# Bucketing an edge list on one core: lane products with the operands exchanged, packed moving rows, and rows turned back to columns by products

## The chip, the cores and the metric

The kernel runs on one core of one Trainium2 chip. The metric is device time in microseconds (us). The engines named here are PE (TensorE: matrix products, with PEld for its weight loads), DVE (VectorE), ACT (ScalarE), POOL (GpSimd) and SP (SyncE, which issues the transfers). In a product the stationary operand is loaded first ("weight load") and the moving operand is streamed past it.

## The reference

Four graph layers over the same 12500 nodes and 200000 edges, sorted by destination, each followed by a residual and a layer norm:

```
edge_index = stack([src, dst])
x = layernorm(x + L0(x, relation_emb, edge_index, edge_type))      # hyperbolic messages, 2 hops, mean per src
x = layernorm(x + L1(x, edge_index, edge_weight, msg_W, gru_...))  # 2 rounds: sum of messages per src, GRU
x = layernorm(x + L2(x, edge_index, W1_l, ...))                    # 2 x (segment_sum(h[src], dst)/deg @ W_l + b + h @ W_r)
x = layernorm(x + L3(x, edge_index, W1_l, ...))                    # the same, wider
```

Each layer gathers node rows by one end of the edges and sums them by the other. The change concerns only the preparation of the edge list, which all four layers use.

## The kernel before

Nodes are cut into 49 groups of 256 (`NG` = 49). An edge belongs to a cell (group of its destination, group of its source), and the program gives each cell 128 lanes. The function `fast` first writes two lists to DRAM: `l_code` (64 x destination group + source group) and `l_pay` (six bf16 numbers an edge: source, destination and edge type within their groups, each plus one, and the edge weight in three parts). Then it runs the **bucketing loop**, `for b in range(NG)`, L910 to L975: one pass for each destination group.

A pass takes a window of 4608 consecutive edges from the sorted list (128 partitions x `WC` = 36 columns) and does the following:

- DVE writes `og` (L919), which says for each edge and each of `GA` = 52 source groups whether it belongs there. Its layout is [partition, group, column], so that the 52 groups of one column lie 36 elements (72 bytes) apart.
- PE counts: `pc` (36 products, L923) the edges per column and group, and `pr` (L929 four products with `upto`, L932 thirty-six with `later`) the rank of each edge among those of its cell. ACT copies `pc` to `per` between the two.
- DVE multiplies `og` by `pr` into `m` (L935), takes the maximum over groups in six steps (L940) and gets `rank`, the lane of each edge. It writes `lane` (L948), which says for each edge and each of 128 lanes whether it goes there, in layout [partition, lane, column], and `v` (L951, six instructions), `og` times each payload number, in layout [partition, payload, group, column].
- PE does the **lane products** `po` (L954): 36 products, one a column, each with `lane[:, :, c]` stationary (128 columns) and `v[:, :, :, c]` moving (6 x 49 = 294 columns), which leaves payloads in [lane, payload x group].
- ACT takes one off (`cols`, L956), POOL writes `slc` and `dlc` (source and destination columns) and DVE adds the three weight parts in `ws`. PE turns `cols` by three transposes to `tr` (L968), ACT copies them to `hr` (L969), and after every seventh pass (`IG` = 7) SP stores `ws` and `hr` to `wgt`, `hop_rows`, `d_rows` and `s_rows` in DRAM.

The tile framework orders the instructions of the loop from its own estimate of costs. Each engine executes its list in order, so passes are interleaved as that order says. The buffers are two deep for `og`, `lane`, `v` and `po`, three for `code` and `pay`, and single for `m`, `pc`, `pr` and `tr`. When the loop is over, a flag is tested, and the layers follow: two hops of the first layer (until about 10.5 ms), then seven passes over all cells (`sum_pass`). They read what the loop has stored, and none of it is edited.

Of the kernel before, what the change touches and what calls it, by code (L numbers as in the profile page):

```python
# [11 lines left out]
F32 = mybir.dt.float32  # L12
BF16 = mybir.dt.bfloat16
I32 = mybir.dt.int32
I16 = mybir.dt.int16
AF = mybir.ActivationFunctionType
OP = mybir.AluOpType
# [6 lines left out]
P = 128  # L24
# [26 lines left out]
F16 = mybir.dt.float16  # L51
# [3 lines left out]
NG = NB // 2  # L55
WC = 36
WIN = WC * P
GA = 52
RC = 9
SMP = 8  # L60
NPAY = 6
# [4 lines left out]
IG = 7  # L66
# [727 lines left out]
@with_exitstack  # L794
def tile_gnn_stack(ctx: ExitStack, tc: tile.TileContext, ins, out: bass.AP):
    fl = ctx.enter_context(tc.tile_pool(name="flag", bufs=1))
    flag = fl.tile([1, 1], I32, name="flag")
    fast(tc, ins, out, flag)
    full = tc.nc.values_load(flag[0:1, 0:1], min_val=0, max_val=P + 1)
    with tc.If(full > 0):  # L800
        general(tc, ins, out)
# [3 lines left out]
def fast(ctx: ExitStack, tc: tile.TileContext, ins, out: bass.AP, flag):  # L805

    nc = tc.nc
    vec, act, pool, pe = nc.vector, nc.scalar, nc.gpsimd, nc.tensor
    tt, ts, stt, copy = vec.tensor_tensor, vec.tensor_scalar, vec.scalar_tensor_tensor, vec.tensor_copy
# [5 lines left out]
    ident = const.tile([P, P], F32, name="ident")  # L815
# [16 lines left out]
    slc = const.tile([P, NG, NG], F16, name="slc")  # L832
    d_cols = dram.tile([P, NG, NG], F16, name="d_cols")
    wgt = dram.tile([P, NG, NG], F32, name="wgt")
    hop_rows = dram.tile([NG, NG, 3, P], F16, name="hop_rows")
    d_rows = dram.tile([NG, NG, P], F16, name="d_rows")
    s_rows = dram.tile([NG, NG, P], F16, name="s_rows")
    l_code = dram.tile([EP * EJ], F32, name="l_code")
    l_pay = dram.tile([NPAY, EP * EJ], BF16, name="l_pay")
    with ExitStack() as st:  # L840
# [43 lines left out]
        wp = st.enter_context(tc.tile_pool(name="bk_w", bufs=2))  # L884
        pp = st.enter_context(tc.tile_pool(name="bk_p", bufs=1, space=PSUM))

        def fixed(name, shape, dtype):
            return sp.tile(shape, dtype, name=name)

        iota_a = fixed("iota_a", [P, GA, WC], F16)  # L890
        pool.iota(iota_a, pattern=[[1, GA], [0, WC]], base=0, channel_multiplier=0, allow_small_or_imprecise_dtypes=True)
        iota_l = fixed("iota_l", [P, P, WC], F16)
        pool.iota(iota_l, pattern=[[1, P], [0, WC]], base=1, channel_multiplier=0, allow_small_or_imprecise_dtypes=True)
        ones_h = fixed("ones_h", [P, WC, P], BF16)
        vec.memset(ones_h, 1.0)
        upto = fixed("upto", [P, P], BF16)
        pool.affine_select(out=upto, in_=ones_h[:, 0, :], compare_op=OP.is_ge, fill=0.0, base=0,
                           pattern=[[1, P]], channel_multiplier=-1)
        later = fixed("later", [WC, WC, P], BF16)
        pool.affine_select(out=later, in_=ones_h[:WC], compare_op=OP.is_gt, fill=0.0, base=0,  # L900
                           pattern=[[1, WC], [0, P]], channel_multiplier=-1)
        unit = fixed("unit", [P, 2 * WC - 1], BF16)
        vec.memset(unit, 0.0)
        vec.memset(unit[:, WC - 1 : WC], 1.0)
        dlc = fixed("dlc", [P, NG, NG], F16)
# [4 lines left out]
        for b in range(NG):  # L910
            at = nc.sync.value_load(begin[0:1, b : b + 1], min_val=0, max_val=EP * EJ - WIN)
            code = wp.tile([P, WC], F32, name="code", bufs=3)
            nc.sync.dma_start(out=code, in_=l_code[ds(at, WIN)].rearrange("(p c) -> p c", p=P))
            pay = wp.tile([P, NPAY, WC], BF16, name="pay", bufs=3)
            nc.sync.dma_start(out=pay, in_=l_pay[:, ds(at, WIN)].rearrange("f (p c) -> p f c", p=P))
            ga = wp.tile([P, WC], F16, name="ga")
            ts(ga, code, -64.0 * b, None, OP.add)
            og = wp.tile([P, GA, WC], BF16, name="og")
            tt(og, iota_a, ga.unsqueeze(1).to_broadcast([P, GA, WC]), OP.is_equal)  # L919

            pc = pp.tile([WC, GA], F32, name="pc")
            for c in range(WC):
                pe.matmul(pc, unit[:, WC - 1 - c : 2 * WC - 1 - c], og[:, :, c], start=c == 0, stop=c == WC - 1)  # L923
            per = wp.tile([WC, GA], BF16, name="per")
            act.copy(per, pc)
            pr = pp.tile([P, WC // RC, 512], F32, name="pr")
            prv = pr[:, :, 0 : RC * GA].rearrange("p h (c a) -> p h c a", a=GA)
            for h in range(WC // RC):
                pe.matmul(prv[:, h], upto, og[:, :, h * RC : (h + 1) * RC].rearrange("p a c -> p c a"),  # L929
                          start=True, stop=False, skip_group_check=True)  # L930
                for c in range(RC):
                    pe.matmul(prv[:, h, c, :], later[:, h * RC + c, :], per, start=False, stop=c == RC - 1,  # L932
                              skip_group_check=True)
            m = wp.tile([P, GA, WC], F16, name="m", bufs=1)
            tt(m.rearrange("p a (h c) -> p a h c", c=RC), og.rearrange("p a (h c) -> p a h c", c=RC),  # L935
               prv.rearrange("p h c a -> p a h c"), OP.mult)
            n = GA
            while n > 1:
                k = n // 2
                tt(m[:, 0:k, :], m[:, 0:k, :], m[:, n - k : n, :], OP.max)  # L940
                n -= k
            rank = wp.tile([P, WC], F16, name="rank")
            copy(rank, m[:, 0, :])
            tt(top, top, rank, OP.max)
            junk = wp.tile([P, WC], F16, name="junk")
            ts(junk, rank, 0.5, None, OP.is_gt, OP.add, accum_out=found[:, b : b + 1])
            lane = wp.tile([P, P, WC], BF16, name="lane")
            tt(lane, iota_l, rank.unsqueeze(1).to_broadcast([P, P, WC]), OP.is_equal)  # L948
            v = wp.tile([P, NPAY, NG, WC], BF16, name="v")
            for f in range(NPAY):  # L950
                tt(v[:, f], og[:, 0:NG, :], pay[:, f, :].unsqueeze(1).to_broadcast([P, NG, WC]), OP.mult)  # L951
            po = pp.tile([P, NPAY, NG], F32, name="po", bufs=2)
            for c in range(WC):
                pe.matmul(po, lane[:, :, c], v[:, :, :, c], start=c == 0, stop=c == WC - 1)  # L954
            cols = wp.tile([P, 3, NG], F32, name="cols")
            act.activation(cols, po[:, 0:3, :], AF.Copy, bias=-1.0)  # L956
            pool.tensor_copy(slc[:, :, b], cols[:, 0, :])
            pool.tensor_copy(dlc[:, b, :], cols[:, 1, :])
            k = b % IG
            if k == 0:  # L960
                ws = wp.tile([P, NG, IG], F32, name="ws")
                hr = wp.tile([NG, IG, 3, P], F16, name="hr")
            act.copy(ws[:, :, k], po[:, 3, :])
            tt(ws[:, :, k], ws[:, :, k], po[:, 4, :], OP.add)
            tt(ws[:, :, k], ws[:, :, k], po[:, 5, :], OP.add)
            tr = pp.tile([NG, 3, P], F32, name="tr")
            for f in range(3):
                pe.transpose(tr[:, f, :], cols[:, f, :], ident)  # L968
            act.copy(hr[:, k], tr)  # L969
            if k == IG - 1:  # L970
                bs = slice(b + 1 - IG, b + 1)
                nc.sync.dma_start(out=wgt[:, :, bs], in_=ws)
                nc.sync.dma_start(out=hop_rows[:, bs, :, :], in_=hr)
                nc.sync.dma_start(out=d_rows[:, bs, :], in_=hr[:, :, 1, :])
                nc.sync.dma_start(out=s_rows[bs, :, :].rearrange("b a p -> a b p"), in_=hr[:, :, 0, :])  # L975

        nc.sync.dma_start(out=d_cols, in_=dlc)

# [517 lines left out]
    with tc.tile_pool(name="c1", bufs=2) as cp:  # L1496
        for c, cs in chunks():
# [4 lines left out]
            r = cp.tile([P, CH, D], F32, name="r")  # L1502
# [12 lines left out]
    dlc = tabs.tile([P, NG, NG], F16, name="dlc")  # L1515
# [74 lines left out]
    for r in range(2):  # L1590
# [4 lines left out]
        with ExitStack() as st:  # L1595
            wp = st.enter_context(tc.tile_pool(name="gru_w", bufs=2))
            pp = st.enter_context(tc.tile_pool(name="gru_p", bufs=1, space=PSUM))
            for b0, n in groups():
                bs = slice(b0, b0 + n)
# [27 lines left out]
                c = wp.tile([P, GB, D], F32, name="c")  # L1627
# [16 lines left out]
    with ExitStack() as l2:  # L1644
# [3 lines left out]
        with ExitStack() as st:  # L1648
            wp = st.enter_context(tc.tile_pool(name="s1_w", bufs=2))
            pp = st.enter_context(tc.tile_pool(name="s1_p", bufs=2, space=PSUM))  # L1650
# [26 lines left out]
        with ExitStack() as st:  # L1677
            wp = st.enter_context(tc.tile_pool(name="s2_w", bufs=2))
            pp = st.enter_context(tc.tile_pool(name="s2_p", bufs=2, space=PSUM))
# [17 lines left out]
    with ExitStack() as st:  # L1697
        wp = st.enter_context(tc.tile_pool(name="t_w", bufs=2))
        pp = st.enter_context(tc.tile_pool(name="t_p", bufs=2, space=PSUM))
        for b0, n in groups():  # L1700
            bs = slice(b0, b0 + n)
# [84 lines left out]
```

## Time and profile before

| | |
|---|---|
| median of 3 runs | 16950.4 us (16940.55 to 16953.64) |
| the profiled execution | 16959.6 us, span 16957.8 us |
| PE busy over the span | 11219.9 us (66%) |
| DVE busy | 13305.5 us (78%) |
| ACT busy | 8790.9 us (52%) |
| first and last lane products of the loop start at | 92.1 and 1621.8 us |
| flag written | 1623.5 us |
| first product of the layers | 1760.4 us |

A line of the profile gives the source line, engine and operation, what is written and read, the number of instructions, then busy time in us and the mean duration of one in ns, and the idle time before them with what ended it. Busy times of PE count overlapping products once, so the busy time over the number of instructions is the spacing of back-to-back products, while the mean is the length of one from start to end. The loop takes up the first tenth of the span.

### The profile page before, as it was taken

Reading aid. Unit: us, or ns where it says so; the run is one execution under the profiler, and the core shown is the slowest. Engines: PE = TensorE matmul, PEld = TensorE weight load, DVE = VectorE, ACT = ScalarE, POOL = GpSimd, SP = SyncE. Lnnn points to the kernel's source line nnn. Section 1 sums busy time; section 2 is a strip of 40 time slices with the busy share of each in tenths; the row PEclk is TensorE's granted clock in tenths of the full one; section 3 lists DMA queues with packets and bytes.
Section 4 is the critical chain, followed back from the end, with each engine's and each line's share of the span. In section 5 each row is a group of like instructions: output and inputs, shape, how many; then the busy total and the mean of one; then the engine's idle time right before and its main releaser. Section 6 shows DMA issues by size and latency. Waiting matters only on the chain. (4 is left out here: it accounts for less than half of the span.)

```text
span 16957.8 us, 370716 instructions
## 1 busy us (share of the span) xinstructions
PE 11219.9 (66%) x148137; PEld 9596.6 (57%) x148137; DVE 13305.5 (78%) x26837; ACT 8790.9 (52%) x25310; POOL 812.7 (5%) x2903
## 2 busy tenths in 40 slices
PE   8997455555555435555555553998999666689997
PEld 3332444444444434444444443886887666688787
DVE  4444899999999979999999998773773789877677
ACT  0000566666666646666666665662663222266565
POOL 0000111111111100000000000000000000000000
PEclk9999877777777767777777776995996555599998
DMA  0001211111111131111111112220220222222122
GB/s 20 6 6 20 80 59 59 61 59 61 59 61 59 52 70 59 59 59 59 60 59 60 59 59 57 81 85 8 88 83 17 81 107 108 81 82 87 58 85 73
DMA packets 427139, 1037.76 MB, mean 61 GB/s; under 512 B 297579, under 2 KB 298102, under 8 KB 387884
## 3 DMA queue, kind: packets, MB, share of 16 engines
q1 hardware_dynamic: 425516, 1014.62, 18.0%
q8 instruction: 1202, 19.69, 0.5%
q14 instruction: 421, 3.45, 0.1%
HBM read 979.68 MB, written 34.85 MB: 60 GB/s over the span
## 5 line engine op out<-in xcount | busy, mean ns | idle before, releaser
L1300 PE MATMUL ph<-hx,o 128*128 128x69 bf16 x28812 | 1728.8, 236 | 4277.8 <-DVE o L1291 3496.8
L1300 PEld LDWEIGHTS <-o 128*128 128x128 bf16 x28812 | 1520.4, 124 | 4506.5 <-DVE o L1291 3627.3
L1551 ACT CAST gb<-pg 128x384 bf16<-128x384 f32 (+2 forms) x5502 | 2607.7, 474 | 2518.9 <-PE pg L1571 2489.7
L1571 PE MATMUL pg<-xs,o 128*128 128x192 bf16 (+2 forms) x28812 | 2956.1, 237 | 637.0 <-DVE o L1564 636.0
L1543 PE MATMUL ps<-gb,s 128*128 128x192 bf16 (+2 forms) x28812 | 2993.1, 238 | 357.6 <-ACT gb L1551 336.5
L1543 PEld LDWEIGHTS <-s 128*128 128x128 bf16 x28812 | 2600.8, 137 | 564.1 <-issue 378.2
L1566 DVE TENSOR_TENSOR s<-iota_r,sc 128x1792 bf16<-128x1792 f16 x2058 | 2507.4, 1223 | 447.9 <-PE ps L1543 422.6
L1571 PEld LDWEIGHTS <-o 128*128 128x128 bf16 x28812 | 2171.0, 105 | 657.0 <-issue 641.8
L1564 DVE TENSOR_SCALAR o<-row,iota_p 128x896 bf16<-128x896 f16 x4116 | 1661.9, 448 | 404.8 <-PE pg L1571 259.8
L1344 ACT ACTIVATE RS<-RS,wtr 128x64 f32<-128x64 f32 x4802 | 1613.4, 336 | 29.5 <-DVE wtr L1258 29.5
L1344 ACT ACTIVATE T<-T,wtr 128x64 f32<-128x64 f32 x4802 | 1613.6, 336 | 18.1 <-DVE wtr L1257 18.1
L1344 ACT ACTIVATE HS<-HS,wh 128x64 f32<-128x64 f32 x4802 | 1612.0, 336 | 3.3 <-DVE wh L1254 3.3
L1305 PE MATMUL pt<-tabx,o 128*128 128x67 bf16 x28812 | 1422.1, 222 | 0.0
L1305 PEld LDWEIGHTS <-o 128*128 128x128 bf16 x28812 | 1363.3, 118 | 0.0
L1382 PE MATMUL ps<-mx,oh 128*128 128x196 bf16 (+1 forms) x9604 | 960.2, 253 | 139.9 <-DVE oh L1376 133.7
L954 PE MATMUL po<-v,lane 128*128 128x294 bf16 x1764 | 985.9, 736 | 20.4 <-DVE lane L948 20.4
L1382 PEld LDWEIGHTS <-oh 128*128 128x128 bf16 x9604 | 839.7, 134 | 153.2 <-DVE oh L1376 150.9
L1336 DVE TENSOR_REDUCE hd<-q 128x7 f32<-128x448 f32 x1372 | 846.8, 617 | 27.2
L1376 DVE TENSOR_TENSOR oh<-iota_r,slc 128x1792 bf16<-128x1792 f16 x686 | 835.7, 1218 | 0.0
L1293 DVE TENSOR_SCALAR o<-row,iota_p 128x1792 bf16<-128x1792 f16 x686 | 781.8, 1140 | 0.0
L954 PEld LDWEIGHTS <-lane 128*128 128x128 bf16 x1764 | 252.6, 146 | 704.5 <-issue 681.6
L1291 DVE TENSOR_SCALAR o<-row,iota_p 128x2688 bf16<-128x2688 f16 x686 | 625.2, 911 | 25.1 <-DMA row<-hop_rows 17.7
(368 smaller groups left out, 14976.7 us busy)
## 6 DMA issues: line engine op xcount, KB each, us to landing
row<-hop_rows SPq DMA_DIRECT2D x686, 672.0 KB
row<-s_rows SPq DMA_DIRECT2D x196, 1568.0 KB
row<-d_rows SPq DMA_DIRECT2D x98, 1568.0 KB
heads<-hx SPq DMA_DIRECT2D x14, 724.5 KB
hx<-heads SPq DMA_DIRECT2D x98, 103.5 KB
tab_h<-H SPq DMA_DIRECT2D x2, 3283.0 KB
res<-t SPq DMA_DIRECT2D x98, 64.0 KB
t<-in_x_dram SPq DMA_DIRECT2D x12, 448.0 KB
```

The costliest lines, as they stand in the source:

```text
L954: pe.matmul(po, lane[:, :, c], v[:, :, :, c], start=c == 0, stop=c == WC - 1)
L1300: pe.matmul(ph[:, t, :], o[:, t, 0, :], head[k][:, q, i * RW : (i + 1) * RW], start=q + i == 0, stop=q + i == 3)
L1305: pe.matmul(pt[:, t, :], o[:, t, 1, :], tabx[:, 2 * (g * HG + t) + q, i * TW : (i + 1) * TW], start=q + i == 0, stop=q + i == 3)
L1336: vec.tensor_reduce(o, q, AX.X, OP.add)
L1344: act.mul(x, x, c[:, g * HG + t : g * HG + t + 1])
L1376: tt(oh, iota_r, slc[:, k, s].unsqueeze(1).to_broadcast([P, GN, HG]), OP.is_equal)
L1382: pe.matmul(ps[k][:, q, :], oh[:, q * P : (q + 1) * P, t], mx[n][:, t, :], start=g + t + q == 0, stop=g * HG + t == HT - 1, skip_group_che ...
L1543: pe.matmul(ps[:, h, :], s[:, h * P : (h + 1) * P, j % HG], gb[:, q, :], start=j + h == 0, stop=j == NG - 1, skip_group_check=True)
L1551: act.copy(gb[:, :n, :], pg[:, :n, :])
L1564: ts(o[:, q, :, :], row[:, j0 : j0 + HG, :], iota_p[:, q : q + 1], None, OP.is_equal)
L1566: tt(s, iota_r, sc[:, k, j0 : j0 + HG].unsqueeze(1).to_broadcast([P, GN, HG]), OP.is_equal)
L1571: pe.matmul(pg[:, len(jobs), :], o[:, q, j - j0, :], xs[:, 2 * j + q, 0:wx], start=q == 0, stop=q == 1)
```

## The change

Four things are edited, all in the bucketing loop.

1. ACT makes a second copy of `og`, `og2`, with the groups of one column side by side; the products of `pc` and the four with `upto` read it instead of `og`.
2. `lane` gets the layout [partition, column, lane]. For this ACT first spreads `rank` over the 128 lanes (`rk`), and DVE compares it with a one-row `iota_l`.
3. The operands of the lane products are exchanged: `v` for two payload numbers (2 x 49 = 98 columns, 36 elements apart) is stationary and `lane[:, c, :]` (128 packed columns) moving; three products a column, 108 a pass. They leave rows, [payload x group, lane].
4. ACT takes these rows to `sb`, and from there to `hr` and `yr` for the stores. Columns are now made by products: one transpose gives source and destination columns, and two products with parts of `ident` and with `halves` (a constant that adds the two remaining weight parts) give the sum of the weights. ACT writes `slc`, `dlc` and `ws` from them. The stores of `hop_rows` become three.

```
-        iota_l = fixed("iota_l", [P, P, WC], F16)
+        iota_l = fixed("iota_l", [P, P], F16)
+        halves = fixed("halves", [2 * NG, NG], F32)
+        tt(halves, ident[: 2 * NG, 0:NG], ident[: 2 * NG, NG : 2 * NG], OP.add)
...
+            og2 = wp.tile([P, WC, GA], BF16, name="og2")
+            act.copy(og2, og.rearrange("p a c -> p c a"))
...
-                pe.matmul(pc, unit[:, WC - 1 - c : 2 * WC - 1 - c], og[:, :, c], start=c == 0, stop=c == WC - 1)
+                pe.matmul(pc, unit[:, WC - 1 - c : 2 * WC - 1 - c], og2[:, c, :], start=c == 0, stop=c == WC - 1)
...
-                pe.matmul(prv[:, h], upto, og[:, :, h * RC : (h + 1) * RC].rearrange("p a c -> p c a"),
-                          start=True, stop=False, skip_group_check=True)
+                pe.matmul(prv[:, h], upto, og2[:, h * RC : (h + 1) * RC, :], start=True, stop=False, skip_group_check=True)
...
-            lane = wp.tile([P, P, WC], BF16, name="lane")
-            tt(lane, iota_l, rank.unsqueeze(1).to_broadcast([P, P, WC]), OP.is_equal)
+            rk = wp.tile([P, WC, P], F16, name="rk", bufs=1)
+            act.copy(rk, rank.unsqueeze(2).to_broadcast([P, WC, P]))
+            lane = wp.tile([P, WC, P], BF16, name="lane")
+            tt(lane, iota_l.unsqueeze(1).to_broadcast([P, WC, P]), rk, OP.is_equal)
...
-            po = pp.tile([P, NPAY, NG], F32, name="po", bufs=2)
+            po = pp.tile([2 * NG, 3, P], F32, name="po", bufs=2)
             for c in range(WC):
-                pe.matmul(po, lane[:, :, c], v[:, :, :, c], start=c == 0, stop=c == WC - 1)
-            cols = wp.tile([P, 3, NG], F32, name="cols")
-            act.activation(cols, po[:, 0:3, :], AF.Copy, bias=-1.0)
-            pool.tensor_copy(slc[:, :, b], cols[:, 0, :])
-            pool.tensor_copy(dlc[:, b, :], cols[:, 1, :])
+                for i in range(3):
+                    pe.matmul(po[:, i, :], v[:, 2 * i : 2 * i + 2, :, c], lane[:, c, :], start=c + i == 0, stop=c == WC - 1,
+                              skip_group_check=True)
...
-            act.copy(ws[:, :, k], po[:, 3, :])
-            tt(ws[:, :, k], ws[:, :, k], po[:, 4, :], OP.add)
-            tt(ws[:, :, k], ws[:, :, k], po[:, 5, :], OP.add)
-            tr = pp.tile([NG, 3, P], F32, name="tr")
-            for f in range(3):
-                pe.transpose(tr[:, f, :], cols[:, f, :], ident)
-            act.copy(hr[:, k], tr)
+            sb = wp.tile([2 * NG, 3, P], F32, name="sb")
+            act.copy(sb, po)
+            act.activation(hr[:, k, :], sb[:, 0, :], AF.Copy, bias=-1.0)
+            act.activation(yr[:, k, :], sb[:NG, 1, :], AF.Copy, bias=-1.0)
+
+            tr = pp.tile([P, 3, NG], F32, name="tr")
+            pe.transpose(tr[:, 0:2, :].rearrange("p f a -> p (f a)"), sb[:, 0, :], ident[: 2 * NG, : 2 * NG])
+            pe.matmul(tr[:, 2, :], sb[:, 1, :], ident[: 2 * NG, NG : 2 * NG], start=True, stop=False)
+            pe.matmul(tr[:, 2, :], sb[:, 2, :], halves, start=False, stop=True)
+            act.activation(slc[:, :, b], tr[:, 0, :], AF.Copy, bias=-1.0)
+            act.activation(dlc[:, b, :], tr[:, 1, :], AF.Copy, bias=-1.0)
+            act.copy(ws[:, :, k], tr[:, 2, :])
             if k == IG - 1:
...
-                nc.sync.dma_start(out=hop_rows[:, bs, :, :], in_=hr)
+                for i, r in enumerate((hr[:NG], hr[NG:], yr)):
+                    nc.sync.dma_start(out=hop_rows[:, bs, i, :], in_=r)
```

More of the change, by code (lines that the diff above doesn't have):

```diff
@@ L891, in fast @@
         pool.iota(iota_a, pattern=[[1, GA], [0, WC]], base=0, channel_multiplier=0, allow_small_or_imprecise_dtypes=True)
-        iota_l = fixed("iota_l", [P, P, WC], F16)
-        pool.iota(iota_l, pattern=[[1, P], [0, WC]], base=1, channel_multiplier=0, allow_small_or_imprecise_dtypes=True)
+        iota_l = fixed("iota_l", [P, P], F16)
+        pool.iota(iota_l, pattern=[[1, P]], base=1, channel_multiplier=0, allow_small_or_imprecise_dtypes=True)
         ones_h = fixed("ones_h", [P, WC, P], BF16)
@@ L961, in fast @@
                 ws = wp.tile([P, NG, IG], F32, name="ws")
-                hr = wp.tile([NG, IG, 3, P], F16, name="hr")
-            act.copy(ws[:, :, k], po[:, 3, :])
-            tt(ws[:, :, k], ws[:, :, k], po[:, 4, :], OP.add)
-            tt(ws[:, :, k], ws[:, :, k], po[:, 5, :], OP.add)
-            tr = pp.tile([NG, 3, P], F32, name="tr")
-            for f in range(3):
-                pe.transpose(tr[:, f, :], cols[:, f, :], ident)
-            act.copy(hr[:, k], tr)
+                hr = wp.tile([2 * NG, IG, P], F16, name="hr")
+                yr = wp.tile([NG, IG, P], F16, name="yr")
+            sb = wp.tile([2 * NG, 3, P], F32, name="sb")
[9 more added lines that the diff above has]
+            act.copy(ws[:, :, k], tr[:, 2, :])
             if k == IG - 1:
@@ L972, in fast @@
                 nc.sync.dma_start(out=wgt[:, :, bs], in_=ws)
-                nc.sync.dma_start(out=hop_rows[:, bs, :, :], in_=hr)
-                nc.sync.dma_start(out=d_rows[:, bs, :], in_=hr[:, :, 1, :])
-                nc.sync.dma_start(out=s_rows[bs, :, :].rearrange("b a p -> a b p"), in_=hr[:, :, 0, :])
+                for i, r in enumerate((hr[:NG], hr[NG:], yr)):
+                    nc.sync.dma_start(out=hop_rows[:, bs, i, :], in_=r)
+                nc.sync.dma_start(out=d_rows[:, bs, :], in_=hr[NG:])
+                nc.sync.dma_start(out=s_rows[bs, :, :].rearrange("b a p -> a b p"), in_=hr[:NG])
         nc.sync.dma_start(out=d_cols, in_=dlc)
```

## The prediction

> **What bounds the kernel now.** Only the bucketing loop (49 windows, start of the program) is edited, so I read busy time by stretches first. Columns: stretch, length, busy time of PE, PEld, DVE, ACT, POOL, granted clock, DMA share, GB/s.
>
> ```profile
> 400.00:600.00 200.00, 193.24 (x741) 71.67 (x741) 92.89 (x152) 6.61 (x24) 3.23 (x12) 1.00 0.08 6
> 1000.00:1200.00 200.00, 192.46 (x748) 72.04 (x748) 86.74 (x139) 6.72 (x24) 2.71 (x12) 1.00 0.04 5
> 1800.00:2000.00 200.00, 101.16 (x2045) 95.77 (x2041) 184.15 (x456) 116.05 (x370) 23.78 (x88) 0.77 0.18 65
> ```
>
> In the loop PE is busy 96% at full clock, DVE under half, ACT 3%; from 1800 us on it is another program, DVE bound. The first lane product starts at 92.1 us, those of the last window at 1602.4: 1510.3/48 = 31.46 us a window. Next, the groups of instructions of the first 2600 us:
>
> ```profile
> L954 PE MATMUL po<-v,lane 128*128 128x294 bf16 x1764 | 985.9, 736 | 20.4 <-DVE lane L948 20.4
> L929 PE MATMUL pr<-og,upto 128*128 128x468 bf16 x196 | 197.1, 1006 | 0.0
> L923 PE MATMUL pc<-og,unit 128*36 128x52 bf16 x1764 | 186.6, 281 | 72.0 <-DVE og L919 72.0
> L932 PE MATMUL pr<-per,later 36*128 36x52 bf16 x1764 | 116.1, 219 | 0.0
> L948 DVE TENSOR_TENSOR lane<-iota_l,rank 128x4608 bf16<-128x4608 f16 x49 | 125.0, 2552 | 0.0
> L951 DVE TENSOR_TENSOR v<-og,pay 128x1764 bf16<-128x1764 bf16 x294 | 310.4, 1069 | 62.8 <-PE po L954 62.8
> L968 PE MATMUL tr<-ident,cols 128*49 128x128 f32 x147 | 42.5, 426 | 7.3 <-ACT cols L956 7.3
> ```
>
> Busy time over 49 is PE's bill for a window: lane products 20.1 us, `upto` 4.0, `pc` 3.8, `later` 2.4, turning 0.9; 31.2 of the 31.46. The timeline shows what one product costs (start, duration):
>
> ```profile
> 802.44 0.14 PEld L954 LDWEIGHTS <-lane 128*128 128x128 bf16 x1 [0.41 <-issue]
> 803.00 0.15 PEld L954 LDWEIGHTS <-lane 128*128 128x128 bf16 x1 [0.41 <-issue]
> 846.25 0.20 PEld L954 LDWEIGHTS <-lane 128*128 128x128 bf16 x2
> 68.35 3.76 PE L923 MATMUL pc<-og,unit 128*36 128x52 bf16 x36 [33.98 <-DVE og L919]
> 91.58 0.43 PEld L932 LDWEIGHTS <-later 36*128 36x128 bf16 x9 [0.83 <-issue]
> ```
>
> A lane product every 0.5535 us for 294 moving columns, a `pc` product every 0.1 for 52: slope 1.875 ns a column. Both read with a step of 36 bf16 = 72 bytes. `upto`, also stepped, takes about 0.94 us for 468 columns: 2.0. Products on packed rows (`later`) follow each other at (0.43-0.1)/8 = 41 ns. The third line is the key to the change: two lane **weight loads**, also stepped by 72 bytes, together last 0.20 us, one of them 0.145, so they start 55 to 65 ns apart.
>
> [...] `v` as stationary operand has 98 columns, [...]; no stepped load of that kind is in this trace. [...]
>
> **The change, part by part.**
>
> *Lane products.* Removed: 36 products, 20.1 us. Added: 108, each a load of 98 columns stepped by 72 bytes and 128 packed moving columns. [...] The load: at 1.875 ns a column 98 x 1.875 = 184 ns, and some 3 ns between two (as 0.1 us exceeds 52 x 1.875): 187. That loads hide behind products is shown by `pc`: 36 stepped products at 100 ns leave no room for their 36-column loads. So 108 x 187 = 20.2 us: the stepped read moves from the moving to the stationary operand and costs what it cost, 98 x 3 being 294. [...]
>
> *Counting products.* `pc` on packed `og2`: 36 at 41 to 46 ns, 1.6 us for 3.8. `upto`: 468 packed columns, 0.2 us for 1.0, so `pr` takes about 2.9 us for 5.7 or so. *Turning:* three fp32 products for three, 0.9 us either way. PE's bill falls to 20.2 + 1.6 + 2.9 + 0.9 = 25.6 us, from 31.2.
>
> *ACT* gains `og2` (1872 elements), `rk` (4608), `sb` (384), and five small ones, and loses `cols`, the old `ws` and `hr`. At 0.833 ns an element plus 0.19 ([...] `pay` L875, 1600 elements in 1.54 us, agrees): 1.75 + 4.0 + 0.5 + 5 x 0.25 to 0.3 + `per` 0.2 = 7.8 us a window, from 1.2. Not a bound by amount, but `og2` and `rk` now stand between DVE and PE.
>
> *DVE* loses two additions (0.48 us) and keeps `lane` at 2.55 (same type and count, both inputs packed): about 12.9 us. *POOL* loses 0.75 us of casts that nothing waited for, and a 4.6 us iota to be had before the loop. *SP* issues two more transfers per seven windows, of 256-byte pieces, ahead of later loads of `code` and `pay`; these are three deep and DVE takes `code` two windows early, so I put nothing; uncovered, each late one costs a few us seven times. The last ones delay the next stage by 1 or 2 us.
>
> *The waits.* In the built order of the new kernel PE repeats over three windows: products of windows n, n+1, n+2 nearly back to back, then `pr`(n+3), `pc`/`pr`(n+4), `pc`/`pr`(n+5), then products of n+3. In between stands a chain through DVE. From the end of products n+2: three quarters of `pr`(n+3) and its end 2.7; `m` 2.1; four `v` of n+4 left to do, put between the steps of the maximum tree, 4.3; tree 1.9; `og` and `ga` of n+5 1.3; `rank`, `top`, `junk` 0.6; `m`(n+4) 2.1; its tree, `og`, `ga`, `rank` 3.4; `lane`(n+3) 2.55: 21.0 us. ACT's chain beside it (`og2`(n+5), `rk`(n+3), `per`(n+5), and then PE's `pr`(n+5)) ends at nearly the same moment. PE works 12 of these 21 and idles 9. Three windows: 3 x 20.2 + 2.7 (two turnings and a part of `pc` among the products) + 21.0 = 84.3, 28.1 us each. Walking the old order by the same durations gives 32.1 for a measured 31.46, so the walk is about 0.6 high.
>
> *Clock.* [...] the stretch at 13400 us, with about 0.6 columns a ns, runs at 0.53. If the loop falls to half clock, the loads stay (stepped less packed load is 33 ns at 0.97 and at 0.53), but `upto` and turning slow down: 0.7 us a window. This and the 0.6 about cancel; I take 28.3.
>
> **Sum.** (31.46 - 28.3) x 48 = 152 us less, filling and draining 2 us more: 150. The profiled execution took 16959.6 us (span 16957.8); it becomes 16810. The median of the runs shown is 9 lower: 16800.
>
> **Rivals.** (1) *Cheap loads*: [...] the chain of 21 us and DVE's 12.9 us take over: about 17 us a window, 690 less, 16260. For it: nothing here measures such a load. [...] 0.12; something between, to 16640, 0.06. (2) *Slower*: the weight loads can't be hidden, or cost more than moving reads. A window gains 0.108 us per ns of a product, so the change loses from about 215 ns (2.2 ns a column). [...] For it: `upto` reads at 2.0 already; against: `pc`. 0.18. (3) *Nothing measurable* (within 0.2%, 34 us, about what this measurement can tell): 200 ns a product at half clock, or ACT reading `og` with 72-byte steps at 1.9 ns an element (`og2` 3.5 us, 1 us a window) on top of the forecast. 0.08. (4) *No effect at all* because another engine bounds the loop: excluded, PE has 96%.
>
> **How the numbers follow.** Forecast 0.56, its own range 16700 to 16900: loads of 175 to 197 ns, `og2` up to 3.5 us. Below it (1), 0.18 in all. 16640 to 17080 holds the forecast, (3), most of (2) and a little of the between: 0.79. Faster 0.74, same 0.08, slower 0.18.
>
> **What will show it.** A load of `v` lasting about 0.26 us (0.08 + 184 ns), products 187 ns apart, `po` busy near 20 us a window: the first step. `pc` 41 to 46 ns, `upto` 0.2 to 0.4 apart. PE busy near 89%, its idle time ended by `lane`, `og2` or `m`: the chain. Clock 1.0 or below. ACT near 8 us a window. From the flag on, the same durations, all of it 150 us earlier. Wrong if products come at under 150 or over 215 ns, or if the gaps of PE are not those 9 us per three windows.

## The result, and the profile after

The changed kernel takes 16802.3 us (median of 4 runs, 16800.0 to 16813.7) against 16952.0 us: a ratio of 0.9914, interval 0.9897 to 0.9931. The forecast was 16800. That the figure fits so closely is partly luck: two terms of the sum were wrong by 3 us per three windows each, in opposite directions, and the loop itself saved more than the whole program did.

Busy time by stretch in the changed kernel (stretch, length, PE, PEld, DVE, ACT, POOL, granted clock, DMA share, GB/s):

```profile
300.00:1300.00 1000.00, 916.24 (x6753) 843.32 (x6752) 498.19 (x721) 328.75 (x324) 0.00 (x0) 1.00 0.10 7
```

PE, at 96% before, is at 92% by this count, and its weight loads have gone from a third of the time to 84%. ACT has risen from 3% to 33%. The groups of instructions of the loop:

```profile
L960 PE MATMUL po<-lane,v 128*98 128x128 bf16 x5292 | 929.0, 379 | 9.7 <-DVE lane L953 9.7
L960 PEld LDWEIGHTS <-v 128*98 128x98 bf16 x5292 | 925.7, 268 | 12.1 <-issue 9.2
...
L951 ACT COPY rk<-rank 128x4608 f16<-128x4608 f16 x49 | 197.8, 4036 | 64.7 <-DVE rank L946 60.6 <-DVE lane L953 4.1
...
L923 ACT COPY og<-og 128x1872 bf16<-128x1872 bf16 x49 | 174.7, 3568 | 173.1 <-DVE og L921 145.0 <-DVE ga L919 28.1
...
L953 DVE TENSOR_TENSOR lane<-iota_l,rk 128x4608 bf16<-128x4608 f16 x49 | 125.1, 2554 | 27.8 <-ACT rk L951 27.8
L933 PE MATMUL pr<-og,upto 128*128 128x468 bf16 x196 | 112.0, 571 | 0.5 <-DVE m L938 0.5
...
L927 PE MATMUL pc<-og,unit 128*36 128x52 bf16 x1764 | 93.6, 222 | 123.8 <-ACT og L923 123.8
```

The lane products, 985.9 us before, are 929.0 us now: three times as many products at 175.5 ns each (929.0/5292), with the loads busy for practically all of it. The counting products have become cheap (`pc` 186.6 to 93.6 us, `upto` 197.1 to 112.0). In their place stands idle time, in which `pc` waits for the copy `og2` (the profile prints it as og): 123.8 us, of which 37.5 us lie ahead of the first count of the program and 74.7 us (15 waits of 5.0 us) between the first lane product and the last. From the first to the last lane product the loop took 1529.7 us before (92.1 to 1621.8) and takes 1357.3 (92.6 to 1449.9): 172 us less. The spans differ by 156 only, since what follows took 15352 us instead of 15336. Its program is the same, and in the other kernels below it took 15340 to 15367 us; where these 16 us come from is not shown.

One repetition of three windows, on PE (start, length, instructions, idle time before them):

```profile
576.75 23.55 PE L960 MATMUL po<-lane,v 128*98 128x128 bf16 x134
```

```profile
618.23 18.54 PE L960 MATMUL po<-lane,v 128*98 128x128 bf16 x106
636.70 0.57 PE L935 MATMUL pr<-per,later 36*128 36x52 bf16 x9
637.20 0.57 PE L933 MATMUL pr<-og,upto 128*128 128x468 bf16 x1
637.71 0.57 PE L935 MATMUL pr<-per,later 36*128 36x52 bf16 x9
...
652.26 1.72 PE L927 MATMUL pc<-og,unit 128*36 128x52 bf16 x36 [5.02 <-ACT og L923]
...
656.29 0.55 PE L935 MATMUL pr<-per,later 36*128 36x52 bf16 x9 [1.81 <-ACT per L929]
...
660.72 24.59 PE L960 MATMUL po<-lane,v 128*98 128x128 bf16 x140
```

From 576.75 to 660.72 are 83.97 us (forecast 84.3). Up to 636.70 PE does three windows of lane products with a few small pieces between them, 59.95 us (forecast 63.3). Then come 24.0 us of counting and waiting (forecast 21.0), of which PE idles 6.8. An `upto` starts 0.50 us before the `later` behind it, where 0.2 to 0.4 was forecast. ACT in that gap:

```profile
648.64 3.57 ACT L923 COPY og<-og 128x1872 bf16<-128x1872 bf16 x1 [5.19 <-DVE og L921]
652.09 4.05 ACT L951 COPY rk<-rank 128x4608 f16<-128x4608 f16 x1
656.02 0.21 ACT L929 CAST per<-pc 36x52 bf16<-36x52 f32 x1
```

This is the chain that the prediction named beside DVE's: `og2`, `rk`, `per`, one after another on one engine, with PE waiting for the first and the last, and DVE's `lane` for `rk` (1.46 us at 656.17).

### The profile page after: what moved, and what is told of

Same layout as the page of the kernel before. It is cut to its first block, busy times and chain, and to the rows that moved or that the text cites. A ratio compares the mean times of both kernels' runs of the same rounds, so it can differ in the third digit from the quotient of the medians.

```text
span 16801.9 us, 377962 instructions
## 1 busy us (share of the span) xinstructions
PE 10995.6 (65%) x151763; PEld 10208.7 (61%) x151763; DVE 13308.1 (79%) x26740; ACT 9184.5 (55%) x25555; POOL 765.4 (5%) x2805
## 5 line engine op out<-in xcount | busy, mean ns | idle before, releaser
L960 PE MATMUL po<-lane,v 128*98 128x128 bf16 x5292 | 929.0, 379 | 9.7 <-DVE lane L953 9.7
L960 PEld LDWEIGHTS <-v 128*98 128x98 bf16 x5292 | 925.7, 268 | 12.1 <-issue 9.2
L956 DVE TENSOR_TENSOR v<-og,pay 128x1764 bf16<-128x1764 bf16 x294 | 301.7, 1073 | 591.4 <-PE po L960 591.4
```

Source lines behind the costliest of these rows:

```text
L960: pe.matmul(po[:, i, :], v[:, 2 * i : 2 * i + 2, :, c], lane[:, c, :], start=c + i == 0, stop=c == WC - 1, skip_group_check=True)
```

## The experiments

### The width of the weight load: 128 and 112 columns

The prediction counts a stepped read at 1.875 ns a column, whichever operand it feeds, and the changed kernel comes to 1.79 (175.5/98). Yet in the kernel before, two stepped loads of `lane` with 128 columns start 55 to 65 ns apart. That 98 columns of `v` would not load as fast as those was the author's estimate, which no product of that trace shows. If the width makes the difference, a load of 128 columns should be much faster than one of 98, and a load of 112 slower. The stationary operand is widened with neighbouring columns of `v`, whose result rows are not used:

```
+            vw = v.rearrange("p f a c -> p (f a) c")
...
-                    pe.matmul(po[:, i, :], v[:, 2 * i : 2 * i + 2, :, c], lane[:, c, :], ...
+                    a0 = min(2 * i * NG, NPAY * NG - W)          # W = 128, or 112
+                    pe.matmul(po[:, i, :], vw[:, a0 : a0 + W, c], lane[:, c, :], ...
```

(`po`, `sb` and `halves` get W rows; the last start is moved back so that the slice ends with `v`.) Expected with 128:

> The changed kernel with the stationary operand of each lane product widened from 98 to 128 columns of v (still 72 bytes apart; the 30 extra rows of the result are not used). Theory (a stepped weight load costs about 1.75 ns a column [...]): [...] products 60 to 66 ns apart instead of 175, lane products 7 us a window instead of 19, the chain through DVE and ACT then bounds the loop at about 17 us a window instead of 28.0: 16250 to 16350 us. The packed counting products should also speed up if PE has been at half clock. Rival (the load costs by columns whatever their number): 128 x 1.75 + 4 = 228 ns, 5.7 us a window more, about 17070.

and with 112:

> The same with 112 columns instead of 128. Theory: a load of 112 x 1.75 + 4 = 200 ns, 24 ns more than with 98, 2.6 us a window, about 16930 us. Rival ([...] the 175 ns is a fixed price per product): products stay at 175 ns or become shorter, 16800 or less.

Measured: 16195.8 us with 128 (ratio 0.9555, 0.9539 to 0.9571), and 16950.7 us with 112, from a single execution. The groups with 128 columns:

```profile
L964 PE MATMUL po<-lane,v 128*128 128x128 bf16 x5292 | 356.0, 232 | 13.6 <-DVE lane L955 10.5 <-DVE v L958 3.0
L964 PEld LDWEIGHTS <-v 128*128 128x128 bf16 x5292 | 351.6, 147 | 17.2 <-issue 10.6 <-DVE v L958 4.6
```

and with 112, over the first 1500 us, which hold 4976 of the 5292:

```profile
L964 PE MATMUL po<-lane,v 128*112 128x128 bf16 x4976 | 997.4, 403 | 2.1 <-DVE lane L955 2.1
```

A product with 112 columns takes 997.4/4976 = 200 ns, as expected to the nanosecond; 14 columns more cost 25 ns, 1.78 each. With 128 it takes 67 ns on average. So between 98 and 112 columns the price of a stepped load goes by columns, and the load is fast with 128 columns and not with 112 or 98; no other width was run. The kernel with 128 beats both kernels by far, and one number did it: the loop shrinks to 758 us (92.3 to 850.4), 15.7 us a window where 17 was expected, so the time lies below the 16250 to 16350 us of the expectation.

The same run answers a question about the clock. PE in two places of its loop:

```profile
428.62 6.60 PE L964 MATMUL po<-lane,v 128*128 128x128 bf16 x106
...
435.48 0.37 PE L935 MATMUL pr<-og,upto 128*128 128x468 bf16 x1
435.78 0.39 PE L937 MATMUL pr<-per,later 36*128 36x52 bf16 x9
...
445.86 0.57 PE L935 MATMUL pr<-og,upto 128*128 128x468 bf16 x1
446.37 0.57 PE L937 MATMUL pr<-per,later 36*128 36x52 bf16 x9
```

and the granted clock (the third number from the end) around them:

```profile
415.00:436.00 21.00, 20.81 (x337) 20.06 (x334) 17.76 (x19) 8.06 (x15) 0.00 (x0) 1.00 0.67 18
440.00:455.00 15.00, 5.90 (x77) 3.85 (x78) 14.25 (x23) 4.70 (x6) 0.00 (x0) 0.50 0.08 9
```

After dense lane products, at 61 ns each here ((6.60 - 0.22)/105), `upto` takes 0.37 us with the next instruction 0.30 behind it, and nine `later` take 0.39; after a pause both take 0.57, with a granted clock of 0.50. The changed kernel has 0.57 throughout (`upto` 551 to 574 ns): by these durations its PE was at half clock, although the column for its loop says 1.00.

By the same measure, so was PE in the loop of the kernel before. The first line is from that kernel, the second from the kernel before with `og2` alone, which is tested further below; each gives least, middle and greatest duration of one product in ns, then the first and last start:

```profile
L932 PE MATMUL pr<-per,later x1764: 217/218/224, 73.0 to 1594.8; 36*128 36x52 bf16 x196
L931 PE MATMUL pr<-og,upto x196: 548/571/574, 73.7 to 1558.9; 128*128 128x468 bf16 x196
```

In the kernel with 128 columns, which has both durations of nine `later` (0.57 and 0.39 us), one takes 205 ns on average (the mean of 1764). In the old loop none takes less than 217, although the column reads 1.00 there as well. So the full clock that the prediction read off, and the fall to half clock that it allowed for, are both misreadings: by these durations the loop ran at half clock before the change and after it.

### Step or width: packed columns of v

```
-            v = wp.tile([P, NPAY, NG, WC], BF16, name="v")
+            v = wp.tile([P, WC, NPAY, NG], BF16, name="v")
...
-                tt(v[:, f], og[:, 0:NG, :], pay[:, f, :].unsqueeze(1).to_broadcast([P, NG, WC]), OP.mult)
+                tt(v[:, :, f, :], og2[:, :, 0:NG], pay[:, f, :].unsqueeze(2).to_broadcast([P, WC, NG]), OP.mult)
...
-                    pe.matmul(po[:, i, :], v[:, 2 * i : 2 * i + 2, :, c], lane[:, c, :], ...
+                    pe.matmul(po[:, i, :], v[:, c, 2 * i : 2 * i + 2, :], lane[:, c, :], ...
```

> The changed kernel with v laid out column by column, so that the 98 stationary columns are packed; DVE then writes v from og2 with the payload number spread over the inner dimension, at about 1.9 us instead of 1.07. Theory (the step of 72 bytes makes the load slow): products 56 ns apart, or 107 if PE is at half clock, window 19 to 22 us, 16400 to 16520. Rival (98 columns are slow to load, packed or not): products stay at 175 ns or so and the slower v makes it 16850 or more.

Measured: 16533.1 us, from a single execution, 13 us above the expected range and far below its rival.

```profile
L956 DVE TENSOR_TENSOR v<-og,pay 128x1764 bf16<-128x1764 bf16 x294 | 582.7, 1989 | 53.8 <-issue 29.5 <-ACT og L923 24.2
L960 PE MATMUL po<-lane,v 128*98 128x128 bf16 x5292 | 384.4, 247 | 334.7 <-DVE lane L953 334.7
```

98 packed columns: 73 ns a product on average, against 175.5 stepped. The average mixes two clocks. In one group of lane products, two stretches of 3 us (length, busy time and products of PE, PEld, DVE, ACT, POOL, granted clock, DMA share, GB/s):

```profile
619.00:622.00 3.00, 3.00 (x31) 3.00 (x30) 3.00 (x4) 0.00 (x0) 0.00 (x0) 0.50 0.03 5
623.00:626.00 3.00, 3.00 (x58) 3.00 (x56) 3.00 (x5) 0.00 (x0) 0.00 (x0) 1.00 0.00 0
```

Without the three or four products already under way at the start of a stretch, these are 28 and 54 in 3 us: 107 ns a product at a granted clock of 0.50 and 56 at 1.00, both as expected. So it is the step that costs: at the half clock of the changed kernel, 175.5 ns with a step stand against 107 without. The 128 moving columns alone account for about 106 of these 107, an estimate from the 43 ns of a `pc` product of 52 packed columns in the changed kernel, so the packed load adds next to nothing. The slower `v` (1.99 us instead of 1.07, six times a window) loads DVE more, and PE idles 334.7 us waiting for its `lane`, which hides part of the gain.

### One part alone

Without `og2` (counting products read `og` as before, the rest as changed):

```
-            og2 = wp.tile([P, WC, GA], BF16, name="og2")
-            act.copy(og2, og.rearrange("p a c -> p c a"))
```

> The changed kernel without og2: pc and upto read og with 72-byte steps as before; the exchanged lane products, rk and the turning by products stay. Theory (the exchange itself is nearly neutral, the gain comes from packed counting): PE has 19.0 + 3.6 + 5.8 + 0.9 = 29.3 us a window and hardly idles, 29.5 to 30 us, about 16870; 70 to 90 us below the kernel before and as much above the changed one. Rival (the exchange carries the gain, the copy only adds a chain): at or below the changed kernel, 16800 or less.

The kernel before with these two lines and the packed counting products alone:

> The kernel before with og2 alone: packed counting products, lane products with the old operands, old columns and transposes. Theory: PE has 20.1 + 1.7 + 4.0 + 0.9 = 26.7 us a window, plus up to 2 us idle while og2 (3.57 us on ACT) stands between og and pc: 27 to 29 us, 16740 to 16840; the packed counting alone gives all or more of the measured gain. Rival (the exchange carries it): above 16870.

Measured: 16879.8 us without `og2` (ratio 0.9940, 0.9923 to 0.9957), 16945.9 us with it alone (0.9981, 0.9974 to 0.9987); the kernel before took 16976.9 us beside them. Busy time by stretch, first without `og2`:

```profile
600.00:800.00 200.00, 200.00 (x1289) 175.34 (x1289) 89.95 (x134) 38.09 (x50) 0.00 (x0) 1.00 0.12 6
```

then `og2` alone, with two groups of its instructions:

```profile
600.00:800.00 200.00, 177.88 (x750) 62.47 (x749) 90.18 (x140) 28.88 (x34) 3.17 (x14) 1.00 0.11 6
```

```profile
L921 ACT COPY og<-og 128x1872 bf16<-128x1872 bf16 x49 | 176.1, 3593 | 307.2 <-DVE m L942 173.1 <-DVE og L919 105.8 <-DVE ga L917 28.3
...
L925 PE MATMUL pc<-og,unit 128*36 128x52 bf16 x1764 | 93.9, 222 | 203.8 <-ACT og L921 203.8
```

Of the first expectation the time nearly held: 97 us below the kernel before, where 70 to 90 were expected. Its theory, that the exchange is nearly neutral, did not hold, for the changed kernel gains 150 us in all. The exchange alone, from first to last lane product, takes 108 us off the loop (1421.9 us): products 20.1 to 18.9 us a window, and PE's idle time, 1.1 us a window before (193 of 200 busy), gone; (1.2 + 1.1) x 48 = 110. Why this idle time is gone is not shown. The second expectation failed, and its rival was the nearer: `og2` alone takes off 36 us of the loop and 0.19% in all. PE's work falls as expected (in the three stretches from 400 to 1000 us it is busy for 521.5 of 600, 26.7 us of a window of 30.7), but it idles 4.0 us a window where I allowed 2. In 3.2 of these `pc` waits for `og2` (61.6 us of the same 600; the 203.8 us above count the wait at the start of the program too). The kernel before is busy for 577.6 us of these 600, 30.3 us of a window of 31.46, so the copy lightens PE by 3.6 us a window. On its own it gives back most of what it buys. Added to the exchange it buys 64 us of the loop (172 - 108), 1.35 of these 3.6 us a window.

### How much of the copy is on the chain

```
-            act.copy(og2, og.rearrange("p a c -> p c a"))
+            act.copy(og2.rearrange("p c a -> p a c"), og)
```

> The changed kernel with the copy og2 on ACT running in the order of its input: packed reads, writes 104 bytes apart, where the changed kernel reads 72 bytes apart and writes packed (3.57 us). Theory (the stepped read is what costs 1.8 ns an element, stepped writes are free): the copy takes 1.75 us, the chain between two groups of lane products is 1.8 us shorter per three windows, 29 us in all: 16773. Rival (stepped writes cost as much): 3.5 us and no change, 16802. Rival (the copy is not on the chain): the copy is shorter and the time is the same.

Measured: 16953.1 us (ratio to the kernel before 0.9998, 0.9989 to 1.0007), so all of the gain is gone. None of the three expectations had the size right: stepped writes are not free, and with this step they cost more than the stepped reads that they replace. The copy over the first 1500 us, and PE in the gap of one repetition:

```profile
L923 ACT COPY og<-og 128x1872 bf16<-128x1872 bf16 x48 | 409.4, 8538 | 168.2 <-DVE og L921 139.2 <-DVE ga L919 28.9
```

```profile
631.62 1.72 PE L927 MATMUL pc<-og,unit 128*36 128x52 bf16 x36 [9.91 <-ACT og L923]
...
643.99 0.98 PE L927 MATMUL pc<-og,unit 128*36 128x52 bf16 x19 [4.88 <-ACT og L923]
644.90 1.48 PE L960 MATMUL po<-lane,v 128*98 128x128 bf16 x7
```

Written with a step of 104 bytes the copy takes 8.54 us, not 3.57 and not 1.75. That makes it a sharper test of the chain than intended. The copy is 4.97 us longer, and the loop (103.0 to 1604.8) is 144.5 us longer, 3.0 us a window or 9 us in three windows: close to twice 4.97. PE shows both: its first wait for the copy grows from 5.02 to 9.91 us, and a second one of 4.88 appears, right before the lane products, where the changed kernel's second copy (656.1 to 659.7 us) is ready just in time for the `pc` products at 659.8. So in the changed kernel one copy of three sets the gap and a second is on the verge of it. A copy as short as forecast would have taken at most 1.8 us off three windows, an estimate from the two durations that no run shows.

### Deeper buffers

`og` and `og2` three deep, `rk` and `m` two, in the kernel with 128 columns and in the changed kernel:

```
-            og = wp.tile([P, GA, WC], BF16, name="og")
+            og = wp.tile([P, GA, WC], BF16, name="og", bufs=3)      # og2 alike; rk, m: bufs 1 -> 2
```

> The kernel with 128-column loads, and og and og2 three deep, rk and m two deep instead of one. DVE works 13.5 us of each 15.65 us window there. Theory (what is left is the chain og, og2, pc, pr, m, rank, rk, lane between the windows, held by these buffers): the window falls towards DVE's 13.5 us, 14 to 15 us, 16110 to 16165. Rival (the single pr in PSUM and the order of the lists hold it, or DVE alone): no change, 16196.

> The changed kernel with the same deeper buffers. PE idles 2.3 us of each 27.9 us window. Theory: some of that goes, 0.5 to 2 us a window, 16710 to 16780. Rival (the idle time stems from the order, in which DVE's work for the next windows stands ahead of m and lane): no change within 20 us of 16802.

Measured: 16225.2 us (0.9569, 0.9553 to 0.9585) and 16836.6 us (0.9925, 0.9908 to 0.9942): no gain in either, the last lane product 27 and 30 us later than without. Both theories fail; the rivals are nearer, but said no change, and the second run lies 34 us above 16802 where 20 were allowed. So giving these four buffers another slot does not shorten PE's waits. More slots change the framework's order too, so the test does not separate the order from the single `pr` in PSUM. A third candidate was left as it was: `v` is two deep in all of these kernels. In the changed kernel DVE stands still for most of its idle time because it waits for lane products before it can write the next `v`:

```profile
L956 DVE TENSOR_TENSOR v<-og,pay 128x1764 bf16<-128x1764 bf16 x294 | 301.7, 1073 | 591.4 <-PE po L960 591.4
```

One such wait, of 14.0 us, ends at 636.81, just as the gap of the repetition shown above begins, and the rest of DVE's list stands behind it. (With 128 columns these waits come to 28.8 us only.) A deeper `v` was not run, and which of the three holds PE stays open. The second run also bears on the clock column. Its PE in the loop, and its `upto`:

```profile
600.00:800.00 200.00, 182.51 (x1318) 170.30 (x1318) 92.42 (x130) 61.59 (x68) 0.00 (x0) 0.51 0.10 7
```

```profile
L933 PE MATMUL pr<-og,upto x196: 371/571/574, 69.5 to 1429.6; 128*128 128x468 bf16 x196
```

The median duration is that of the changed kernel (571 ns), where the column reads 1.00, and here the profile grants 0.51.

## Why the prediction was right, point by point

- **PE bounds the loop, and only the loop changes.** Right. From the flag on, the kernel does what it did, though 16 us slower. But PE was not as full as 31.2 of 31.46 us: the busy times of the groups overlap where one follows another, and the stretches of 96% are 30.3 us, with 1.1 idle.
- **The stepped read moves to the stationary operand and costs what it cost.** Right in kind, and its rivals fell: the loads hide the products (loads busy for 925.7 us, products for 929.0), and of the three widths tried only 128 is fast. On PE only a step of 72 bytes was run. Measured were a load of 268 ns (forecast 0.26 us) and products at 175.5 ns (forecast 187). The term was 6% too high: 1.79 ns a column instead of 1.875 and 3 ns between; 108 x 11.5 ns = 1.24 us a window better.
- **Counting products.** `pc` as forecast: (1.72 - 0.22)/35 = 43 ns. `pr` was mis-sized: 4.0 us a window and not 2.9, because `upto` at half clock stands 0.50 us ahead of its successor. The prediction took the granted clock of 1.00 at its word and mixed two clocks: its 41 ns for a packed product came from `later` in a loop that was already at half clock, so `pc` came out right, while the 0.2 us for `upto` was an estimate for full clock that no product of the trace before shows; with 128 columns, at a granted clock of 1.00, 0.30 from start to start was measured. Half clock was allowed for, with 0.7 us a window, but as a fall that the change might bring; there was no fall.
- **ACT.** `rk` right (4.03 for 4.0 us). `og2` was the worst term: 3.57 us for 1.75. I applied the rate of packed elements (0.833 ns and 0.19 us, as in 1.54 us for the 1600 elements of `pay` and 4.03 for the 4608 of `rk`) to a read with 72-byte steps. The trace says 1.8 ns an element (3.38 us beyond the same 0.19, over 1872) and decides. I had kept 3.5 us only as a bound, within rival (3).
- **The chain.** Right in shape: three groups of lane products, then a gap, with `og2`, `rk` and `per` on ACT nearly as long as DVE's part. Forecast 21.0 us with 9 idle, measured 24.0 with 6.8. The longer `og2` makes ACT's side the longer one, and slower counting fills more of the gap.
- **The sum.** 3 x 20.2 + 2.7 + 21.0 = 84.3 became 59.95 + 24.0 = 83.97. The products came out 3.3 us too high and the gap 3.0 too low. Both errors are in the account, and neither was forecast to cancel. I then took 28.3 us a window for a walk of 28.1; measured 27.9 to 28.0, so the loop saved 172 us instead of 150, and the 16 us by which the rest took longer made up most of that.
- **Where the gain was placed.** Here the prediction was wrong, though not in its number: it put all of PE's saving down to packed counting and none to the exchange. Alone, the counting gains 0.19% and the exchange 0.60%, of 0.86% together. In the total, lane products 1.2 us a window cheaper than forecast stand against a `pr` that is 1.1 us dearer, so that the time came out is luck in this part.
- **Rivals.** The slower case (from 215 ns a product) did not come, but was near, and begins earlier than forecast: 112 columns, at 200 ns, lose all but a trace of the gain. That is what rival (3) had said of 200 ns at half clock. Cheap loads, rival (1), came true only when I made them, at 128 columns: 16196 us beside its worked-out 16260.

## What to carry to other kernels

When a product reads an operand with a step, exchanging the operands can move the price without removing it: with 72-byte steps a column cost 1.875 ns as moving operand here and 1.79 as stationary one. Count columns times the stepped rate on whichever side is slower, and see whether a weight load can be brought to 128 columns, even by loading columns that nobody needs: here 128 were fast (67 ns a product), and 98 and 112 were not (175.5 and 200 ns). Before crediting a lighter PE, write down the order of one repetition and see which engine stands between two groups of products: a relayout copy on an idle engine can still give back most of what it buys, as `og2` alone did (PE's work 3.6 us a window less, 36 us in all off the loop). For such a copy, take the duration from a row with the same step, not from packed rows (here 3.57 us, where the rate of packed rows had forecast 1.75). And check the clock by the duration of a product that is known, before a time from one kernel is used in another.

## What the runs showed of the hardware that I had not expected

- A product with a weight load in 72-byte steps and 128 packed moving columns: 98 columns 175.5 ns and 112 columns 200 ns, both beside an `upto` of 571 ns; 128 columns 61 ns at a granted clock of 1.00, with `upto` at 0.37 us. With 98 packed columns it takes 107 ns at a granted clock of 0.50 and 56 at 1.00.
- ACT, copying 1872 bf16: 3.57 us reading with 72-byte steps and writing packed, 8.54 us reading packed and writing with 104-byte steps (about 4.5 ns an element).
- PE, busy nearly all the time, showed the durations of half clock: in the changed kernel (92% busy, lane products 175.5 ns apart) `upto` takes 571 ns, against 0.37 us after products 61 ns apart, and in the kernel before (96% busy, lane products 553.5 ns apart) `later` takes 218 ns throughout. What about these products leaves the clock at half is not shown. The granted clock read 1.00 for such a stretch in the changed kernel and 0.51 in the one with deeper buffers, with a median `upto` of 571 ns in both, so it is the duration of a known product that tells.
